# Layer 1's weight tiles at the end of a two-layer graph kernel: one of four made by GpSimd instead of VectorE

## The chip, the cores and the metric

The kernel runs on one core of a Trainium2 chip. The metric is the device time of one launch in microseconds. The engines are named as in the profile: PE is TensorE, with PEld its weight load; DVE is VectorE, ACT is ScalarE, POOL is GpSimd, and SP is SyncE, which here only issues transfers.

## The reference

Eight batches of 2048 nodes with 256 features pass through two layers over one adjacency matrix. After each layer comes a residual sum and a layer norm.

```python
# layer 0: attention within chunks of 256 keys, 4 heads of 64
scores = clip(einsum('bhnd,bhjcd->bhnjc', q, kc) / sqrt(64), -10, 10)
scores = where(mask == 0, -10.0, scores)
attn = softmax(scores, axis=-1)
ctx = einsum('bhnjc,bhjcd->bhnd', attn, vc)
out = layernorm(ctx @ Wo.T + bo + x) * gamma + beta
x = layernorm(x + out)
# layer 1: graph attention over all nodes, 4 heads of 64
Wh = (x @ W).reshape(B, N, 4, 64)
e = s_src[:, :, None, :] + s_dst[:, None, :, :]
e = where(e > 0, e, 0.2 * e)
e = where(adj != 0, e, -inf)
alpha = softmax(e, axis=2)
x = layernorm(x + elu(einsum('bijh,bjhd->bihd', alpha, Wh)))
```

## The kernel before

All tensors are in float32, apart from the masks, which are bytes. The order of instructions on every engine is written out by hand (a manual schedule): each engine runs its instructions in the order in which the program emits them, and waits only for what it needs.

**Layer 0** of a batch is a loop of 64 slots. A slot makes two tiles of scores on PE (L377), clips and masks them on DVE from PSUM into two `pr` buffers of 128 x 1024 (L388), takes the exponential on ACT (L400), multiplies by the values on PE (L412), and copies the result out on ACT (L419). POOL divides by the sums and adds up (L434 into `part` or `acc`, L436). The `pr` pool has four buffers.

**Layer 1** of a batch is cut into 12 units: three bands of 6, 5 and 5 blocks of 128 target nodes (`BANKS`), times four heads. A unit has 16 weight tiles, one for each block j of 128 source nodes. A tile is 128 x 768 in the first band and 128 x 640 in the others. The exponential of the leaky sum has been factored, so that a tile `e` is the maximum of a row `srow` (the same on all partitions) and a scalar `gd` per partition, times the adjacency bytes `et`. One DVE instruction makes it (L734), in `Layer1.make`. `Layer1.use` then takes the tile as the weights of 12 or 10 matrix products with `waug` (L754), which the profile records as 24 or 20. The `e` pool has four buffers. The bytes come by SP transfers of four tiles each (L716, `JG = 4`, three buffers), the rows by one transfer per unit (L705, two buffers).

When a unit is done, `close` takes the reciprocal of its sums on DVE (`dn`, L777 and L778), scales on ACT (`hh`, L782), applies the pieces of the elu (`ee` and `hp`, L786 and L788), and joins them on DVE (L790).

Layer 1 of batch b runs beside layer 0 of batch b + 1: `Layer1.step`, called once in each slot, makes and uses three tiles, with the tiles made three ahead of their use. For the last two batches this differs:

- In batch 7's layer 0 the last 14 slots (`LATE`) make no step of batch 6's layer 1. Those 14 steps are emitted afterwards, between the pieces that finish batch 7's layer 0 (output product, two norms, values for layer 1, and `factors`, whose last piece scales `waug` on POOL at L681).
- Layer 1 of batch 7 then runs with no layer 0 beside it: 64 steps of three tiles. Between them the final norms of batch 6 and of most of batch 7 are done: sum (L815), statistics (L477, L480), `rs_c` and `off_c` (L485 and L486 on DVE, L487 and L488 on POOL), and the scaled output `o` on ACT (L492), which SP stores (L821).

Of the kernel before, what the change touches and what calls it, by code (L numbers as in the profile page):

```python
# [8 lines left out]
F32 = mybir.dt.float32  # L9
# [5 lines left out]
ALU = mybir.AluOpType  # L15
AX = mybir.AxisListType

P = 128
CH = 512
# [3 lines left out]
def adj_resnorm_kernel(  # L23
# [19 lines left out]
    nc = tc.nc  # L43
# [26 lines left out]
    WIDE = max(BANKS)  # L70
    JG = 4
# [4 lines left out]
    prp = ctx.enter_context(tc.tile_pool(name="prp", bufs=4))  # L76
    ep = ctx.enter_context(tc.tile_pool(name="ep", bufs=4))
# [3 lines left out]
    small = ctx.enter_context(tc.tile_pool(name="small", bufs=2))  # L81
# [117 lines left out]
    class Masks:  # L199
# [3 lines left out]
        def __init__(self):  # L203
            self.pieces = [
                (QT * q + u, m) for q in range(NCH) for m in range(len(BANKS)) for u in range(QT)
            ]
            self.raw, self.bits, self.done = [], [], []
            self.next = 0
# [152 lines left out]
    def load_slab(s):  # L361
        q, hp, c = where[s]
        slab = slabs.tile([P, KT, CH], I8, tag="slab", name="slab")
        nc.sync.dma_start(out=slab, in_=clipD[q][:, KT * c : KT * (c + 1), :])
        slab_of[s] = slab

    def scores(s):
        q, hp, c = where[s]
        slab = slab_of.pop(s)
        cols = slice(q * CH, (q + 1) * CH)  # L370
        pss = []
        for u in range(KT):
            t = KT * c + u
            ps = two_banks([P, 2, CH], "ps")
            for k in range(2):
                rows = slice(k * D, (k + 1) * D)
                nc.tensor.matmul(  # L377
                    ps[:, k, :],
                    lhsT=kT[rows, hp, t * P : (t + 1) * P],
                    rhs=qT[rows, hp, cols],  # L380
                    start=True,
                    stop=True,
                )
            pss.append(ps)
        probs[s] = []
        for u in range(KT):
            pr = prp.tile([P, 2, CH], F32, tag="pr", name="pr")
            nc.vector.scalar_tensor_tensor(  # L388
                pr,
                pss[u],  # L390
                -CLIP,
                slab[:, u, :].unsqueeze(1).to_broadcast([P, 2, CH]),
                op0=ALU.max,
                op1=ALU.min,
            )
            probs[s].append(pr)

    def exps(s, u):
        pr = probs[s][u]
        nc.scalar.activation(pr, pr, AF.Exp, scale=0.125)  # L400
# [289 lines left out]
    class Layer1:  # L690
        def __init__(self, b, gd, waug):
            self.b, self.gd, self.waug = b, gd, waug
            self.made = self.used = 0
            self.rows, self.edge, self.e = {}, {}, {}
            self.tail = []
            self.load_edge(0)
            self.load_edge(1)
            self.load_row(0)
# [22 lines left out]
        def make(self):  # L721

            if self.made == TILES:
                return
            k = self.made
            n, j = k // NT, k % NT
            m, h = UNITS[n]
            if j == NT // 2:
                self.load_row(n + 1)
            if j % JG == 0:  # L730
                self.load_edge(k // JG + 2)
            w = BANKS[m] * P
            e = ep.tile([P, WIDE * P], F32, tag="e", name="e")
            nc.vector.scalar_tensor_tensor(  # L734
                e[:, :w],
                self.rows[n][:, :w],
                self.gd[:, h, j : j + 1],
                self.edge[k // JG][:, j % JG, :w],
                op0=ALU.max,
                op1=ALU.mult,  # L740
            )
            self.e[k] = e
            self.made += 1

# [160 lines left out]
    lower = None  # L905
    for b in range(B):
# [15 lines left out]
        for s in range(SLOTS):  # L922
            q, hp, c = where[s]
            i = s % QS
# [93 lines left out]
        if b + 1 < B:  # L1018
            (k0, v0, q0), (l1, t1, k1, v1, q1), (l2, t2, k2, v2, q2), (l3, t3, k3, v3, q3) = turns
            rest = [lambda: lower.rest(1)] if lower else []  # L1020
            first = [] if b else [lambda: before.values((1,))]
            order = [begin, *rest, l1, *rest, *first, lambda: before.values((2, 3))]
            order += [*rest, ctx, *rest, k0]
            order += [steps[0], t1, steps[1], v0, steps[2], steps[3], l2, k1, steps[4], q0]
            order += [steps[5], v1, t2, l3, steps[6], q1, steps[7], k2, steps[8], steps[9], t3, v2]
            order += [lambda: [load_slab(s) for s in range(3)], fs[0], q2, fs[1], k3, fs[2], v3]
            order += [lambda: scores(0), q3, lambda: [exps(0, u) for u in range(KT)]]
        else:

            step = lower.step  # L1030
            order = [begin, lambda: before.values((2, 3)), steps[0], step, ctx, step, steps[1], step]
            order += [steps[2], step, steps[3], step, steps[4], step, steps[5], step, steps[6], step]
            order += [steps[7], step, steps[8], step, steps[9], step, fs[0], step, fs[1], step, fs[2]]
            order += [step, lambda: lower.rest(4)]
            assert sum(p is step for p in order) == LATE
# [4 lines left out]
        lower = Layer1(b, gd, waug)  # L1040

    closing, ending = Closing(B - 2, CLOSING_ALONE), Closing(B - 1, ENDING)
    closing.do(-1)
    for _ in range(STEP):
        lower.make()
    for s in range(SLOTS + 1):
# [50 lines left out]
```

## Time and profile before

| | us |
|---|---|
| median of 3 runs (3795.84 to 3798.59) | 3796.66 |
| the profiled execution | 3792.69 |
| its span | 3790.9 |

| engine | busy us | share of the span | instructions |
|---|---|---|---|
| PE | 3678.4 | 97% | 72100 |
| DVE | 3195.5 | 84% | 4810 |
| ACT | 1946.8 | 51% | 3601 |
| POOL | 1387.7 | 37% | 1202 |

The profile is one execution. A row of a group has the line, the engine, the operation, output and inputs with their shapes, and the count; then busy time in all and the mean of one in ns; then the engine's idle time just ahead of these instructions and what ended it. A row of the timeline has the start in us from the beginning of the span, the length, the engine, the line and the count.

### The profile page before, as it was taken

Reading aid. Unit: us, or ns where it says so; the run is one execution under the profiler, and the core shown is the slowest. Engines: PE = TensorE matmul, PEld = TensorE weight load, DVE = VectorE, ACT = ScalarE, POOL = GpSimd, SP = SyncE. Lnnn points to the kernel's source line nnn. Section 1 sums busy time; section 2 is a strip of 40 time slices with the busy share of each in tenths; the row PEclk is TensorE's granted clock in tenths of the full one; section 3 lists DMA queues with packets and bytes.
Section 4 is the critical chain, followed back from the end, with each engine's and each line's share of the span. In section 5 each row is a group of like instructions: output and inputs, shape, how many; then the busy total and the mean of one; then the engine's idle time right before and its main releaser. Section 6 shows DMA issues by size and latency. Waiting matters only on the chain. (4 is left out here: it accounts for less than half of the span.)

```text
span 3790.9 us, 160217 instructions
## 1 busy us (share of the span) xinstructions
PE 3678.4 (97%) x72100; PEld 2747.7 (72%) x72100; DVE 3195.5 (84%) x4810; ACT 1946.8 (51%) x3601; POOL 1387.7 (37%) x1202
## 2 busy tenths in 40 slices
PE   9999999999999999999999999999999999999787
PEld 5656677776777777776777767777677777776676
DVE  5876499986999689995999959998699968998798
ACT  4666355545555555554555545555555555555221
POOL 1445234333444344333443324433344434434310
PEclk9999999999999999999999999999999999999899
DMA  6652334333343343433433434333333333343354
GB/s 164 152 114 67 76 102 105 100 82 113 106 105 101 89 120 98 104 96 87 137 86 104 102 99 126 105 100 82 113 106 104 101 88 120 98 104 81 97 152 120
DMA packets 756545, 398.50 MB, mean 105 GB/s; under 512 B 425744, under 2 KB 721040, under 8 KB 755856
## 3 DMA queue, kind: packets, MB, share of 16 engines
q1 hardware_dynamic: 705856, 354.54, 36.6%
q10 hardware_dynamic: 50000, 33.70, 2.8%
q8 instruction: 564, 9.24, 1.0%
q14 instruction: 125, 1.02, 0.1%
HBM read 331.22 MB, written 56.89 MB: 102 GB/s over the span
## 5 line engine op out<-in xcount | busy, mean ns | idle before, releaser
L388 DVE SCALAR_TENSOR_TENSOR pr<-ps,slab 128x1024 f32<-128x1024 f32 x1024 | 1191.3, 1204 | 199.2 <-PE ps L377 195.1
L734 DVE SCALAR_TENSOR_TENSOR e<-srow,gd,et 128x640 f32<-128x640 f32 (+1 forms) x1536 | 1342.6, 930 | 10.1 <-PE pa L754 5.4
L412 PEld LDWEIGHTS pc<-vaug,pr 128*64 128x64 f32 x32768 | 1039.7, 138 | 411.2 <-issue 303.6
L412 PE MATMUL pc<-vaug,pr 128*64 128x65 f32 x32768 | 1156.3, 224 | 17.6 <-ACT raw L419 10.0
L754 PE MATMUL pa<-waug,e 128*64 128x65 f32 x32768 | 1080.5, 224 | 39.6 <-DVE e L734 37.8
L400 ACT ACTIVATE pr<-pr 128x1024 f32<-128x1024 f32 x1024 | 1044.9, 1056 | 71.2 <-DVE pr L388 60.3
L754 PEld LDWEIGHTS pa<-waug,e 128*64 128x64 f32 x32768 | 1020.7, 139 | 63.8 <-DVE e L734 37.6
L377 PE MATMUL ps<-qT,kT 64*128 64x512 f32 x4096 | 1025.7, 617 | 3.3 <-DVE pr L388 2.4
L419 ACT COPY raw<-pc 128x260 f32<-128x260 f32 x1024 | 384.8, 376 | 1235.7 <-PE pc L412 1196.2
L434 POOL TENSOR_TENSOR part<-raw,rd 128x512 f32<-128x512 f32 x448 | 467.9, 1044 | 1424.5 <-DVE rd L427 1410.2
L377 PEld LDWEIGHTS ps<-qT,kT 64*128 64x128 f32 x4096 | 350.3, 186 | 328.1 <-issue 222.6
L436 POOL TENSOR_TENSOR acc<-acc,part 128x512 f32<-128x512 f32 x448 | 574.9, 1283 | 35.2
L427 DVE RECIPROCAL rd<-raw 128x8 f32<-128x8 f32 x512 | 100.5, 196 | 102.4 <-ACT raw L419 100.7
L434 POOL TENSOR_TENSOR acc<-raw,rd 128x512 f32<-128x512 f32 x64 | 66.7, 1043 | 317.4 <-DVE rd L427 316.6
L782 ACT ACTIVATE hh<-pa,dn 128x64 f32<-128x64 f32 x512 | 114.7, 322 | 101.5 <-DVE dn L778 101.5
L571 PE MATMUL pw<-w_sb,x1T 128*128 128x264 f32 x512 | 140.9, 411 | 9.2 <-DVE x1T L283 8.7
L487 POOL TENSOR_TENSOR rs_c<-rs_c,nhalf 128x4 f32<-128x4 f32 x32 | 55.6, 1737 | 229.6 <-DVE off_c L486 229.6
L321 PE MATMUL pp<-xT,wk_sb 128*128 128x512 f32 x256 | 118.6, 607 | 7.9 <-ACT qT L329 6.6
L527 PE MATMUL po<-wo_sb,qT 128*128 128x256 f32 x512 | 125.0, 389 | 1.1 <-DVE qT L454 0.8
L321 PE MATMUL pp<-xT,wq_sb 128*128 128x512 f32 x256 | 116.2, 596 | 0.0
L337 PE MATMUL pv<-wv_sb,xT 128*128 128x256 f32 x512 | 115.9, 379 | 0.0
L571 PEld LDWEIGHTS pw<-w_sb,x1T 128*128 128x128 f32 x512 | 92.9, 194 | 30.9 <-DVE x1T L283 9.3
(93 smaller groups left out, 1857.3 us busy)
## 6 DMA issues: line engine op xcount, KB each, us to landing
et<-edgeD SPq DMA_DIRECT2D x256, 320.0 KB, 3.1
slab<-clipD SPq DMA_DIRECT2D x512, 128.0 KB, 3.3
et<-edgeD SPq DMA_DIRECT2D x128, 384.0 KB, 3.4
srow<-rowD SPq DMA_DIRECT2D x64, 320.0 KB, 4.2
xg<-in_x_dram SPq DMA_DIRECT2D x32, 512.0 KB, 5.1
x1D<-y ACTq DMA_DIRECT2D x32, 512.0 KB, 4.2
x1g<-x1D SPq DMA_DIRECT2D x32, 512.0 KB, 5.3
out_dram<-o SPq DMA_DIRECT2D x32, 512.0 KB, 3.7
```

Source lines behind the costliest of these rows:

```text
L321: nc.tensor.matmul(pps[c], lhsT=w[:, kc, c * P : (c + 1) * P], rhs=st["xT"][:, kc, :], start=(kc == 0), stop=(kc == KC - 1),)
L377: nc.tensor.matmul(ps[:, k, :], lhsT=kT[rows, hp, t * P : (t + 1) * P], rhs=qT[rows, hp, cols], start=True, stop=True,)
L388: nc.vector.scalar_tensor_tensor(pr, pss[u], -CLIP, slab[:, u, :].unsqueeze(1).to_broadcast([P, 2, CH]), op0=ALU.max, op1=ALU.min,)
L400: nc.scalar.activation(pr, pr, AF.Exp, scale=0.125)
L412: nc.tensor.matmul(pc[z * D : (z + 1) * D, i, :], lhsT=probs[s][u][:, k, i * P + z * D : i * P + (z + 1) * D], rhs=vaug[:, KT * c + u, 2 * ...
L419: nc.scalar.copy(raws[s][:, k], pc)
L434: nc.gpsimd.tensor_mul(part, raw[:, :, :, :D], rd.to_broadcast([P, 2, QT, D]))
L436: nc.gpsimd.tensor_add(accv, accv, part)
L527: nc.tensor.matmul(po[:, k, :], lhsT=qT[:, c, t * P : (t + 1) * P], rhs=wo_sb[:, c, :], start=(c == 0), stop=(c == KC - 1),)
L571: nc.tensor.matmul(pw[:, k, : F + 2 * H], lhsT=self.x1T[:, c, u * P : (u + 1) * P], rhs=w1_sb[:, c, :], start=(c == 0), stop=(c == KC - 1),)
L734: nc.vector.scalar_tensor_tensor(e[:, :w], self.rows[n][:, :w], self.gd[:, h, j : j + 1], self.edge[k // JG][:, j % JG, :w], op0=ALU.max, ...
L754: nc.tensor.matmul(self.pa[z * D : (z + 1) * D, i * D1 : (i + 1) * D1], lhsT=e[:, i * P + z * D : i * P + (z + 1) * D], rhs=self.waug[:, j ...
```

## The change

A flag `shared` is added to `Layer1`. It is set for batch 6's layer 1 just before its last 14 steps are emitted, and for batch 7's layer 1 before its first tile. While it is set, the tiles with j % 4 = 2 are made in another way: ACT copies the bytes into floats, in a buffer of the `pr` pool that layer 0 no longer uses; POOL takes the maximum of the row and the scalar, in the buffer of `part`; and POOL multiplies the two. The other three of four tiles are made as before. The tile `e` of the shared ones takes no buffer of the `e` pool.

```diff
             w = BANKS[m] * P
-            e = ep.tile([P, WIDE * P], F32, tag="e", name="e")
-            nc.vector.scalar_tensor_tensor(
-                e[:, :w],
-                self.rows[n][:, :w],
-                self.gd[:, h, j : j + 1],
-                self.edge[k // JG][:, j % JG, :w],
-                op0=ALU.max,
-                op1=ALU.mult,
-            )
+            row, edge = self.rows[n][:, :w], self.edge[k // JG][:, j % JG, :w]
+            scalar = self.gd[:, h, j : j + 1]
+            if self.shared and j % JG == 2:
+
+                e = prp.tile([P, 2, CH], F32, tag="pr", name="eg").rearrange("p k i -> p (k i)")
+                nc.scalar.copy(e[:, :w], edge)
+                top = small.tile([P, WIDE * P], F32, tag="part", name="top", bufs=1)
+                nc.gpsimd.tensor_scalar(top[:, :w], row, scalar, None, ALU.max)
+                nc.gpsimd.tensor_mul(e[:, :w], e[:, :w], top[:, :w])
+            else:
+                e = ep.tile([P, WIDE * P], F32, tag="e", name="e")
+                nc.vector.scalar_tensor_tensor(
+                    e[:, :w], row, scalar, edge, op0=ALU.max, op1=ALU.mult
+                )
...
+            lower.shared = True
             step = lower.step
...
     closing.do(-1)
+    lower.shared = True
     for _ in range(STEP):
         lower.make()
```

More of the change, by code (lines that the diff above doesn't have):

```diff
@@ L693, in __init__ @@
             self.made = self.used = 0
+            self.shared = False
             self.rows, self.edge, self.e = {}, {}, {}
```

## The prediction

> **What bounds the kernel now.** I read the engine shares and the slices first, then the stretches at the end, then groups, waits and the order of time there. On the page PE is busy for 97% of the span and DVE for 84%; the change touches only tiles made after layer 0 has run out of work, so what counts is the last 270 us. The view by stretches gives, for each: length, busy us and instructions of PE, weight load, DVE, ACT, POOL, then granted clock, DMA share and GB/s.
>
> ```profile
> 3520.00:3585.00 65.00, 49.85 (x1004) 43.82 (x1000) 50.90 (x85) 19.34 (x53) 20.91 (x14) 0.88 0.34 99
> 3585.00:3662.00 77.00, 62.10 (x1580) 55.45 (x1582) 76.44 (x122) 15.02 (x40) 10.99 (x9) 0.90 0.47 143
> 3662.00:3775.00 113.00, 100.12 (x2520) 85.68 (x2520) 110.72 (x173) 20.67 (x68) 3.78 (x4) 0.97 0.49 135
> ```
>
> From 3585 to 3775 (the last batch's 192 weight tiles, alone) DVE is busy for 187 of 190 us, PE for 162, ACT for 36, POOL for 15. The groups and waits of 3590 to 3775 name the work: 188 tiles by L734 on DVE, with no idle time ahead of them, and PE waiting on them and on hardly anything else.
>
> ```profile
> L734 DVE SCALAR_TENSOR_TENSOR e<-srow,gd,et 128x640 f32<-128x640 f32 x128 | 103.2, 876 | 0.0
> L734 DVE SCALAR_TENSOR_TENSOR e<-srow,gd,et 128x768 f32<-128x768 f32 x60 | 56.6, 1009 | 0.0
> ...
> PE pa L754 <- DVE e L734: 23.1, 27, 3.6
> ```
>
> The rows of the timeline give the pace (start, length, engine, line, count):
>
> ```profile
> 3632.15 8.43 DVE L734 SCALAR_TENSOR_TENSOR e<-srow,gd,et 128x768 f32<-128x768 f32 x9
> 3633.20 8.35 PE L754 MATMUL pa<-waug,e 128*64 128x65 f32 x216 [0.29 <-DVE e L734]
> ...
> 3719.57 7.22 DVE L734 SCALAR_TENSOR_TENSOR e<-srow,gd,et 128x640 f32<-128x640 f32 x9
> 3720.48 7.17 PE L754 MATMUL pa<-waug,e 128*64 128x65 f32 x180 [0.27 <-DVE e L734]
> ```
>
> So in a row a tile costs DVE 7.22/9 = 0.80 us at 640 wide and 8.43/9 = 0.94 at 768, and PE 0.80 and 0.93. DVE sets the end here, PE is close behind: with DVE wholly free of the bound, only PE's 23 us of waiting could go.
>
> **What the Trainium skill says.** "SBUF — State Buffer", Who interferes with whom: a DVE instruction with two inputs in SBUF contends with a GpSimd instruction that reads SBUF; the shared pair of ports is an exclusive lock for the whole instruction, and the second to issue "fully blocks". L734 has two such inputs, the row srow and the bytes et. L388, layer 0's big DVE step, has one (ps lies in PSUM), so layer 0 tells nothing on this. "GPSIMD Engine Reference", Elementwise — side-by-side cycle accounting: about 2.6 cycles an element at 1.2 GHz for two inputs, 1.03 for a light one-input body, about 1.8 for a tight loop.
>
> The trace of before agrees on the lock, where waug is scaled on POOL beside L734. A POOL multiply of 1024 takes 1.90 us undisturbed (minimum of its line), a tile of 640 takes 0.84 to 0.88:
>
> ```profile
> 3575.43 0.88 DVE L734 SCALAR_TENSOR_TENSOR e<-srow,gd,et 128x640 f32<-128x640 f32 x1
> 3576.42 2.48 POOL L681 TENSOR_TENSOR waug<-waug,ed 128x1024 f32<-128x1024 f32 x1
> 3577.06 2.52 DVE L734 SCALAR_TENSOR_TENSOR e<-srow,gd,et 128x640 f32<-128x640 f32 x1
> ```
>
> The multiply that starts at 3576.42 ends at 3578.90, some 1.8 us after the tile ahead of it (about 3577.1); the tile issued at 3577.06 ends at 3579.58, 0.68 us after the multiply. Neither shares: they take turns, a POOL instruction held the pair for about its own time less 0.1 (its start-up overlaps the wait), and a tile behind one costs 0.68 instead of 0.80 (I take 0.82 for 0.94 at 768). The same stands at 3527, where a tile took 1.67 us beside a POOL multiply.
>
> **The change part by part.**
>
> Removed: one L734 in four, from the point where the flag is set. The flag comes with 14 steps of batch 6's layer 1 to go: tiles 153 to 191 are then still to be made, 10 of them with j % 4 = 2, all 640 wide. Of the last batch's 192, 48 are: 16 of 768, 32 of 640. DVE's saving alone is 32 x 0.80 + 16 x 0.94 = 40.6 us for the last batch and 8.0 ahead of it.
>
> Added on ACT: 58 copies of bytes into floats. The nearest row, L242's casts (685 ns at 640, 790 at 768), makes 58 of them about 42 us. ACT is busy for 36 of 190 us in the last stage, and needs neither lock nor DVE: I cost them at nothing beside the DVE-POOL turns. If that cover were gone, at most 42 us would show. ACT is in order: behind a copy stand hh, ee and hp of L782 to L788 and the o rows of L492; a copy itself stands behind hh (which waits for dn on DVE) and behind o (which waits for POOL's off_c). Tiles are ordered three ahead of PE, about 2.4 us, so one such wait is mostly borne; I bound it from 0 to 1.5 us at each of six norms, 0 to 9, and take 0.
>
> Added on POOL: 58 maxima and 58 multiplies, all reading SBUF. No row shows a POOL maximum at this shape: by the skill's 1.03 cycles an element plus 0.2 us of start (estimate; the 64-element copy of L679 takes 0.30), 0.75 us at 640 and 0.86 at 768; by 1.8 cycles, 1.14 and 1.33. I take the lower. Multiply: L436, with two full inputs, takes 1283 ns at 512; less 0.18 of start that is 2.15 ns an element, which is the skill's 2.6 cycles; so 1.56 us at 640 and 1.83 at 768. By L434 and L681, with a broadcast input (1044 at 512, 1903 at 1024, 1.68 an element), 1.26 and 1.47. I take the higher. Held less 0.1 each: 2.11 us a tile at 640, 2.49 at 768.
>
> A group of four tiles, DVE and POOL in turns:
> - at 640, before 4 x 0.80 = 3.20; after 0.68 + 0.68 + 0.80 + 2.11 = 4.27, so 1.07 longer;
> - at 768, before 3.75; after 0.82 + 0.82 + 0.94 + 2.49 = 5.07, so 1.32 longer.
>
> Last batch: 32 x 1.07 + 16 x 1.32 = 55 us. Against it stand DVE instructions with fewer than two SBUF tensors, beside which POOL can run: statistics 8.4 + 2.2, rs and off 2.0, dn 4.1, in all 16.7 us; I count half, 8. Leaves 47. The 10 tiles ahead of it: 10 x 1.07 = 11; DVE has 14 of 65 us idle there, so I count 6. Sum **+53 us**.
>
> Moved: eg uses layer 0's pr buffers, four of them, once in four tiles, so a buffer is free 16 tiles later, and its wait costs nothing; e's own four buffers now last 5.3 tiles. top takes part's buffer, used by POOL alone, in order. A transfer of bytes now waits for ACT's read too, and one of rows for POOL's; three byte buffers of four tiles leave room, and the SP queue (et, srow, x1g, out) is paced by the tiles as now: nothing. On POOL rs_c and off_c stand behind up to a maximum and a multiply, about 2.3 us; o behind them isn't wanted at once. The waug multiplies stand behind one tile of batch 6, which PE needs first anyway. The last 15 us (3775 on) have no such tile and stay. PE: 3.2 us of work in 4.27 leaves gaps of about 1 us; the granted clock, 0.90 to 0.97 here now, may dip; PE has room for it.
>
> The profiled execution took 3792.7 us (span 3790.9 and 1.8 around it); 3792.7 + 53 = 3845.7. The median of the runs, 3796.7, is 4 above the profiled time, so I forecast **3850 us**.
>
> **The rivals.**
> - *Turns, at higher prices or with queues in the way.* Maximum at 1.8 cycles: 4.66 and 5.54 us a group, 32 x 1.46 + 16 x 1.79 = 75, nothing covered, 15 ahead, 9 in ACT's queue: about +99, 3895. For it: POOL has no one-input row of this width. I give 0.2.
> - *Turns, cheap.* Multiply by the broadcast rows: 3.97 and 4.71 a group, 32 x 0.77 + 16 x 0.96 = 40, less all 16.7 of cover and nothing ahead: +23, 3820. 0.15.
> - *Faster: PE becomes the bound.* POOL works beside DVE, the group takes PE's 3.2 us, and most of PE's 23 us of waiting goes, with perhaps 5 ahead of it: about 3770. It decides from where both POOL instructions hold the pair for less than one DVE tile and the two shortened ones, 0.80 + 0.24 = 1.04 us at 640. One 512-wide multiply alone takes 1.04, and the 2.52 us tile above speaks against it; for it speaks that POOL runs beside DVE all through layer 0 (L434 at 1044). 0.07.
> - *Nothing to see*, losses and cover cancelling: 0.03.
>
> **How the numbers follow.** The main case has 0.55. Range 3818 to 3895: it spans the cheap and dear ends and leaves out the faster and the level case and a tail above. A measurement of this kernel can tell about 0.2% (8 us) from no change: faster 0.07, same 0.03, slower 0.90.
>
> **What would show it.** L734 falls by 58; surviving tiles of the end have means well over 0.88 and 1.01 us, many at 1.5 to 2.5; POOL's new rows have means above their undisturbed prices; stage 3585 to 3775 grows to about 237 us with DVE still reported nearly full and PE waiting longer for e and eg. Wrong would be: tiles at 0.84 beside POOL rows at full width, or PE waiting for ACT's copies rather than for POOL and DVE.

## The result and the profile after

The change makes the kernel slower: 3864.9 us median (3863.7 to 3868.4) against 3796.3, a ratio of 1.0183 with a 95% interval of 1.0171 to 1.0196, or +68.6 us. The forecast was 3850, with a range of 3818 to 3895.

The page of the changed kernel puts the loss at the very end. These are the busy rows in 40 slices (a digit is the share in tenths), DVE and POOL before, then DVE and POOL after.

```profile
DVE  5876499986999689995999959998699968998798
POOL 1445234333444344333443324433344434434310
...
DVE  5876599977999599995999779995999959986898
POOL 1444234333434244433443334332443424446897
```

In the last four slices POOL is busy for 60% to 90% and more, where it had 40% falling to nothing before, and DVE is no emptier for it. The stretch of the last batch's tiles, from the start of the first to the end of the last product, before and after (length; busy us and instructions of PE, weight load, DVE, ACT, POOL; granted clock, DMA share, GB/s):

```profile
3585.40:3773.80 188.40, 162.21 (x4096) 141.13 (x4096) 186.45 (x293) 35.21 (x105) 14.66 (x12) 0.94 0.48 139
...
3597.40:3846.00 248.60, 161.24 (x4096) 147.05 (x4096) 228.17 (x244) 66.55 (x151) 223.13 (x109) 0.89 0.37 107
```

PE's busy time for its 4096 recorded products is 161 us against 162, so the granted clock, 0.89 instead of 0.94, is not where the time went. A tile has three ways to be late now: DVE, POOL, or ACT's copy. The groups and PE's waits of the last batch (3590 to 3847 us) show which:

```profile
L745 DVE SCALAR_TENSOR_TENSOR e<-srow,gd,et 128x640 f32<-128x640 f32 x96 | 125.0, 1363 | 3.9 <-PE pa L760 3.9
L741 POOL TENSOR_SCALAR top<-srow,gd 128x640 f32<-128x640 f32 x32 | 75.3, 2353 | 3.0
L745 DVE SCALAR_TENSOR_TENSOR e<-srow,gd,et 128x768 f32<-128x768 f32 x48 | 72.8, 1572 | 4.7 <-PE pa L760 4.6
L742 POOL TENSOR_TENSOR eg<-eg,top 128x640 f32<-128x640 f32 x33 | 58.0, 1757 | 4.9 <-issue 1.9 <-POOL top L741 0.4
...
PE pa L760 <- POOL eg L742: 58.6, 37, 8.0
PE pa L760 <- DVE e L745: 33.9, 32, 7.5
```

DVE makes 144 tiles of the last batch instead of 192, but a tile of 640 takes 1363 ns in the mean instead of 876. Its busy time for tiles rose from some 163 us to 198. PE waits 92 us instead of 23, and no wait for ACT's copy is among the waits of that stretch.

One group of four tiles, row by row of the timeline (start, length, engine, line), shows why. In the kernel before, four such tiles took 3.20 us.

```profile
3834.13 1.69 POOL L742 TENSOR_TENSOR eg<-eg,top 128x640 f32<-128x640 f32 x1
3834.36 2.15 DVE L745 SCALAR_TENSOR_TENSOR e<-srow,gd,et 128x640 f32<-128x640 f32 x1
3835.92 2.33 POOL L741 TENSOR_SCALAR top<-srow,gd 128x640 f32<-128x640 f32 x1
3836.43 1.42 DVE L745 SCALAR_TENSOR_TENSOR e<-srow,gd,et 128x640 f32<-128x640 f32 x1
3837.77 0.87 DVE L745 SCALAR_TENSOR_TENSOR e<-srow,gd,et 128x640 f32<-128x640 f32 x1
3838.34 1.69 POOL L742 TENSOR_TENSOR eg<-eg,top 128x640 f32<-128x640 f32 x1
```

The next group begins 4.20 us after this one (3834.13 to 3838.34). Follow the ends. The multiply ends at 3835.82, and the tile issued beside it ends 0.69 later, at 3836.51. The maximum then gets its turn. The next tile ends at 3837.85, and since a tile behind a turn needs 0.68, its turn began at 3837.17: the maximum had kept DVE out for only 0.66 us, though it goes on until 3838.25. The third tile, 0.87 us, runs undisturbed beside the rest of the maximum and ends at 3838.64. Then the second multiply keeps the ports until 3840.03. The turns are 0.69 + 0.66 + 0.68 + 0.79 + 1.39 = 4.21 us. That they add up without a gap follows from how they are counted, each from the end of the one before. What is not by count is how regular they are: in this trace all 30 DVE tiles of 640 that start while a multiply of 640 runs end 0.68 to 0.69 us after it, as the tile at 3834.36 does. With the maximum none does: the tile that waits for it ends some 0.41 us before the maximum's own end.

By stages, in the two profiled executions (72.2 us apart): 3.3 us lie ahead of batch 7's last pieces, before any changed instruction (nothing is changed there in the ten kernels below either, and their profiled executions take 2.0 to 7.9 us longer for it than the one before). From there to the first tiles of the last batch, with 10 shared tiles, it takes 67.7 us instead of 59.0 (+8.7). The last batch's tiles take 248.6 us instead of 188.4 (+60.2). From the last matmul to the end it takes 17 us in both.

### The profile page after: what moved, and what is told of

Its sections match the earlier page's. It is cut to its first block, busy times and chain, and to the rows that moved or that the text cites. A ratio compares the mean times of both kernels' runs of the same rounds, so it can differ in the third digit from the quotient of the medians.

```text
span 3862.8 us, 160403 instructions
## 1 busy us (share of the span) xinstructions
PE 3678.7 (95%) x72100; PEld 2753.8 (71%) x72100; DVE 3237.9 (84%) x4752; ACT 1985.6 (51%) x3659; POOL 1633.5 (42%) x1318
## 5 line engine op out<-in xcount | busy, mean ns | idle before, releaser
L745 DVE SCALAR_TENSOR_TENSOR e<-srow,gd,et 128x640 f32<-128x640 f32 (+1 forms) x1478 | 1374.8, 985 | 22.4 <-PE pa L760 16.6
L760 PE MATMUL pa<-waug,e 128*64 128x65 f32 x31544 | 1037.4, 224 | 38.3 <-DVE e L745 37.3
L760 PEld LDWEIGHTS pa<-waug,e 128*64 128x64 f32 x31544 | 985.6, 140 | 49.9 <-DVE e L745 36.4
L741 POOL TENSOR_SCALAR top<-srow,gd 128x640 f32<-128x640 f32 (+1 forms) x58 | 142.2, 2451 | 4.8
L760 PE MATMUL pa<-waug,eg 128*64 128x65 f32 x1224 | 52.4, 239 | 70.9 <-POOL eg L742 70.9
```

The lines of the kernel that those rows point to most:

```text
L741: nc.gpsimd.tensor_scalar(top[:, :w], row, scalar, None, ALU.max)
L745: nc.vector.scalar_tensor_tensor(e[:, :w], row, scalar, edge, op0=ALU.max, op1=ALU.mult)
L760: nc.tensor.matmul(self.pa[z * D : (z + 1) * D, i * D1 : (i + 1) * D1], lhsT=e[:, i * P + z * D : i * P + (z + 1) * D], rhs=self.waug[:, j ...
```

## Experiments

Two theories lead to a slower kernel. **A, turns:** POOL and DVE take turns at the SBUF ports that they share, so the time of POOL's reads is added to DVE's tiles. **B, POOL's queue:** POOL is simply too slow for one tile in four. In the trace after, both look full (POOL is busy for 223 of the 248.6 us, DVE for 228), so these shares alone do not tell them apart.

### Take the second SBUF input away from DVE: e1_rows_psum, e2_rows_psum_all_dve

```diff
+            near = row
+            if self.alone:
+                if k == 0:
+                    self.bring(0)
+                if j == NT - 4:
+                    self.bring(n + 1)
+                near = self.near[n][:, :w]
...
+        def bring(self, n):
...
+                self.near[n] = two_banks([P, 2, CH], "near").rearrange("p k i -> p (k i)")
+                nc.scalar.copy(self.near[n][:, :w], self.rows[n][:, :w])
...
-                    e[:, :w], row, scalar, edge, op0=ALU.max, op1=ALU.mult
+                    e[:, :w], near, scalar, edge, op0=ALU.max, op1=ALU.mult
```

> The changed kernel, but in the last batch's layer 1 ACT copies each unit's row into PSUM (two banks that layer 0 no longer uses) and DVE's tiles read it there; POOL goes on reading the row in SBUF. A DVE tile then has one SBUF input. Theory A (turns for the shared ports set the pace, 4.20 us a group of four at 640 wide): the tiles fall back to 0.85 to 0.9 us, POOL's maximum and multiply to their undisturbed 1.88 and 1.53, and the pace becomes POOL's own 3.6 us a group at 640, 4.2 at 768: 48 groups 182 us, with 28 us for POOL's norm steps and their waits 210 against 249 in the changed kernel, so about 3826 us. Theory B (POOL's queue by itself sets it, the ports don't matter): 3865, nothing moves. Theory C (only the ports matter): PE's pace, about 3785.

> Control for the run before: the kernel before, all tiles on DVE, with the last batch's rows in PSUM. If a tile costs DVE the same from PSUM (two L388 of 1024 take 2.34 us, as much per element as SBUF to SBUF), 3797 within 5. If PSUM rows cost by themselves, more: 0.06 us a tile for 192 tiles would be 12.

In both, ACT copies each unit's row into PSUM once, and DVE's tiles of the last batch read it there (`near`). e1 took 3816.7 us (3813.3 to 3818.8), a ratio to before of 1.0051 (1.0036 to 1.0066): 48 us less than the changed kernel, by nothing but the place of DVE's row. The control e2 took 3794.9, a ratio of 0.9993 (0.9985 to 1.0002), so PSUM rows by themselves are neither gain nor loss. In e1's timeline the tiles and POOL's instructions have their undisturbed lengths side by side:

```profile
3748.83 1.88 POOL L756 TENSOR_SCALAR top<-srow,gd 128x640 f32<-128x640 f32 x1
...
3750.80 1.54 POOL L757 TENSOR_TENSOR eg<-eg,top 128x640 f32<-128x640 f32 x1
3751.28 0.88 DVE L760 SCALAR_TENSOR_TENSOR e<-near,gd,et 128x640 f32<-128x640 f32 x1
3752.08 0.88 DVE L760 SCALAR_TENSOR_TENSOR e<-near,gd,et 128x640 f32<-128x640 f32 x1
3752.44 1.89 POOL L756 TENSOR_SCALAR top<-srow,gd 128x640 f32<-128x640 f32 x1
```

The group now takes 3.61 us (3748.83 to 3752.44), which is POOL's own 1.88 + 1.54 with two gaps of 0.1. So A holds for the 48 us, and B for a rest: without turns POOL is still slower than PE's 3.2 us. In the profiled executions the last batch takes 200.9 us in e1, 248.6 in the changed kernel and 188.4 before, so 12.5 us of 60.2 are left to B there. The remainder of e1's loss is the 10 early tiles, whose rows e1 leaves in SBUF. A's forecast of 3826 was 9 too high, by the same 9 as its 210 us for the last batch. A theory in which only the ports matter would have put e1 near 3785. e1's waits in the last batch (3600 to 3797 us) agree: PE waits for POOL and hardly for DVE.

```profile
PE pa L775 <- POOL eg L757: 58.8, 46, 2.6
PE pa L775 <- DVE e L760: 0.5, 1, 0.5
```

### Take half of POOL's work away: e3_no_max

```diff
-                top = small.tile([P, WIDE * P], F32, tag="part", name="top", bufs=1)
-                nc.gpsimd.tensor_scalar(top[:, :w], row, scalar, None, ALU.max)
-                nc.gpsimd.tensor_mul(e[:, :w], e[:, :w], top[:, :w])
+                nc.gpsimd.tensor_mul(e[:, :w], e[:, :w], row)
```

> The changed kernel with POOL's maximum left out: POOL multiplies the floats by the row itself, so a shared tile lacks the maximum. Theory A (turns): a group at 640 takes 0.68 + 0.80 + 0.80 + 1.39 = 3.67 us against 3.20 before, at 768 about 4.4 against 3.75: 32 x 0.47 + 16 x 0.65 = 25 us more than before for the last batch and up to 5 ahead of it, less up to 10 of cover: 3810 to 3827. Theory B (POOL's queue alone): POOL needs 1.7 us a group, PE becomes the bound, 3770 to 3785, faster than before.

3823.1 us (3822.2 to 3829.9), ratio 1.0073 (1.0058 to 1.0088), inside A's interval and 38 us or more above B's. POOL has time to spare here and DVE has none, by the groups of the last batch (3605 to 3811 us):

```profile
L743 DVE SCALAR_TENSOR_TENSOR e<-srow,gd,et 128x640 f32<-128x640 f32 x96 | 116.5, 1276 | 0.0
...
L740 POOL TENSOR_TENSOR eg<-eg,srow 128x640 f32<-128x640 f32 x32 | 63.5, 1999 | 54.7 <-ACT eg L739 46.8 <-PE pa L758 7.8
```

The kernel is slower than before although POOL's 32 multiplies have 55 us of idle time ahead of them and DVE has a quarter fewer tiles: the tiles that are left have become half as long again. And the maximum is worth (3864.9 - 3823.1) / 58 = 0.72 us a tile, close to the 0.66 that it kept DVE out and far from its own 1.88. The 0.72 has in it whatever POOL's queue costs besides, so the two agree only roughly.

### ACT's part by itself: e4_act_copies

```diff
-                nc.gpsimd.tensor_scalar(top[:, :w], row, scalar, None, ALU.max)
-                nc.gpsimd.tensor_mul(e[:, :w], e[:, :w], top[:, :w])
-            else:
+            if True:
```

> The kernel before with all tiles on DVE, and ACT's 58 copies of bytes into floats kept, which nothing reads. If ACT's part is free as predicted: 3797 within 3. If copies delay hh, o and with them dn and the norms, up to 42 us (58 x 0.73).

3796.0 us, ratio 0.9997 (0.9988 to 1.0006): the 58 copies cost nothing that can be measured.

### Where, and how many: e5_late_only, e6_one_in_eight

The edits drop the flag for the last batch, or put `j % 8 == 2` for `j % JG == 2`.

> The changed kernel with the sharing only in batch 6's last 14 steps (10 tiles); the last batch's tiles are all on DVE. By the prediction 6 us more than before, by the changed kernel's profile 8.7: 3803 to 3808. If the part ahead of the last batch hides its tiles altogether, 3797.

> The changed kernel with one tile in eight on POOL instead of one in four, rows in SBUF. Theory A (each shared tile adds its turns): half the loss, 3825 to 3835. Theory B (POOL's queue sets the pace only because POOL has too many tiles): POOL needs some 4 us in eight tiles of 6.4, so PE or DVE sets it, and DVE has one tile in eight less: 3780 to 3790.

e5: 3805.5, ratio 1.0025 (1.0016 to 1.0034), so the 10 early tiles cost 9.3 us. e6: 3831.3, ratio 1.0091 (1.0076 to 1.0106), so half of the tiles cost half of the loss: 35 us for 29 tiles, 1.21 each, and 68.6 for 58, 1.18 each. POOL's multiplies of 640 have 45 us of idle time ahead of them in e6, and every shared tile still costs its turns. With B the half would have been a gain.

### From the reason to a faster version: e7 to e10

If turns are the reason, then without them a share small enough for POOL should gain. All four runs have the row for DVE in PSUM and share nothing ahead of the last batch. e7 gives POOL one tile in eight. e8 gives it one in four, but lets ACT make the maximum, as the positive part of row minus scalar, plus the scalar (`neg` is the scalar with its sign turned, made once on DVE):

```diff
-                nc.gpsimd.tensor_scalar(top[:, :w], row, scalar, None, ALU.max)
+                nc.scalar.activation(top[:, :w], row, AF.Relu, bias=neg)
+                nc.scalar.activation(top[:, :w], top[:, :w], AF.Identity, bias=scalar)
```

> The last batch's rows for DVE in PSUM, one tile in eight on POOL, nothing shared ahead of the last batch. Theory A: no turns, POOL has 3.6 us of work in eight tiles of 6.4, DVE seven tiles and its 29 us of norms, 168 us against 188 before: 3775 to 3785. If what is left of the contention (sums and joins with two SBUF inputs, POOL's latency) eats it: 3790 to 3797.

> The last batch's rows for DVE in PSUM, one tile in four shared, nothing shared ahead of the last batch; of the shared tile ACT makes the maximum too (Relu of row minus scalar, then plus scalar), POOL only multiplies. Theory A: POOL 1.6 us, ACT 2.1 us, DVE 2.4 us and PE 3.2 us in a group of four, so PE sets the pace: 3770 to 3780. If ACT's four instructions a group delay dn, hh and the row copies: 3785 to 3800.

e7: **3781.3 us** (3779.6 to 3785.7), ratio 0.9960 (0.9945 to 0.9975), faster than both kernels. e6 has the same share and takes 50 us more; what sets it apart from e7 is its rows in SBUF and five early tiles (half of e5's 9.3 us), so the rows are worth some 45. e8 missed the gain: 3797.5, ratio 1.0003 (0.9994 to 1.0011). Its waits name a ring between ACT and POOL:

```profile
POOL eg L759 <- ACT top L758: 72.7, 35, 4.8
...
ACT top L757 <- POOL eg L759: 21.9, 24, 1.4
```

`top` has one buffer. ACT can't begin the next maximum before POOL has multiplied with this one, and POOL waits for ACT. The period in the timeline is 3.40 us, 0.83 + 0.83 + 1.55 and the handovers. e9 gives `top` two buffers (`tag="acc"`, whose pool holds two). e10 goes on from e7 with three tiles of 16.

> The run with ACT making the maximum, but with two buffers for it instead of one. In the trace of that run ACT's Relu waited for POOL's multiply of the group before, and the multiply for ACT: 0.83 + 0.83 + 1.55 + handovers = 3.40 us a group at 640. If that ring is the cause, PE's 3.2 us sets the pace: 9 to 14 us less, 3783 to 3789. If ACT's order (o, hh and row copies between) is the cause, no change: 3795 to 3800.

> Rows for DVE in PSUM, three tiles of 16 on POOL (j = 2, 7, 12) instead of two, last batch only. In the run with one in eight PE still waited 17 us for DVE. Theory A: DVE has 12 tiles less, 10 us; POOL's 36 tiles take 137 us plus norms: PE sets the pace, 3772 to 3780. If POOL's latency of 3.6 us a tile is late for PE at that spacing: 3782 to 3792.

e9: 3783.0, ratio 0.9966 (0.9954 to 0.9979), 14.5 us less than e8 by the second buffer alone. Whether e7 or e9 is better stays open: in the profiled executions e9's last batch is the shorter, 170.5 us against 177.1 in e7 and 188.4 before, but 7.9 us more than before had gone by in it where nothing was changed.

e10: 3787.6, ratio 0.9976 (0.9970 to 0.9983), no better than e7 and most likely worse (the two intervals overlap a little). Its waits have changed sides: between 3600 and 3775 us PE waits 22.5 us for POOL and 6.3 for DVE, where e7 had 4.5 and 16.7. A POOL tile takes 3.6 us, and PE comes to it after four or five tiles of 0.8 us; POOL also stands 16 us at `rs_c`, waiting for DVE's statistics. That these two make POOL's tile late is read from the waits, no run separates them.

## Why the prediction was right, and where its sizes were off

- **The bound before** (DVE, tiles of 0.80 and 0.94 us) and what could be gained at most were read right: the best version gains 15 us of the 23 that PE waited.
- **The turns** were read right from the few places where POOL worked beside L734. e1 shows the mechanism, e3 and e6 show that POOL's queue is not the main part. The Trainium skill's page "SBUF — State Buffer" (Who interferes with whom) is confirmed on who contends, also on a DVE instruction with one SBUF input being free (e1). Its statement that the lock is held for the whole instruction is not: by the rows above the maximum kept DVE out for 0.66 us of its undisturbed 1.88. The measurement decides. The prediction had named tiles of 0.84 us beside POOL rows as a sign that it was wrong; the third tile of the group above, 0.87 us, is such a tile, beside the second half of the maximum.
- **The price of a group** came out at 4.20 us (forecast 4.27) at 640, and 4.98 at 768, between the maxima that start at 3658.97 and 3663.95 (forecast 5.07). The multiply was priced well: 1.54 us undisturbed at 640, forecast 1.56. The maximum was not: 1.88 where the prediction took 0.75, from a price of 1.03 cycles an element that does not hold for it here. The sum survived by luck: what counts in turns is the time for which DVE is kept out, and 0.66 happened to be near the 0.65 used.
- **The term that was missing is POOL's own queue, and what a late tile of POOL does to DVE.** For the last batch the forecast was 55 us of turns less 8 of cover (statistics beside which POOL can run), 47, all of it in DVE's busy time. That time grew by 41.7 us (186.45 to 228.17). The other 18.5 of the 60.2 are time in which DVE stands idle, 20.4 us instead of 2. For 19.4 of these it waits for PE:

```profile
DVE dn L783 <- PE pa L760: 10.8, 3, 5.8
DVE e L745 <- PE pa L760: 8.6, 2, 4.6
...
POOL rs_c L487 <- DVE off_c L486: 13.7, 4, 5.4
```

Ahead of each of these five waits PE itself had waited for a tile of POOL. In four of them POOL had made the steps `rs_c` and `off_c` of a norm shortly before that tile, and in three it had first stood 3.4 to 5.4 us until DVE's statistics were there. The prediction saw that these steps would wait behind a tile, and put that at nothing; it did not see that the tiles behind them would wait too. With a maximum of 1.88 us POOL's chain is 1.88 + 1.54 + 0.2 = 3.6 us a tile undisturbed, which leaves it little to catch up with: it was busy or waiting at `rs_c` for 237 of 248.6 us. That the long maximum is what used up its slack is argued from these numbers, no run isolates it.
- **The tiles ahead of the last batch**: 6 forecast, 9.3 measured (e5); the idle time of DVE there covered almost nothing of the 11.
- **ACT's copies and the moved buffers at nothing**: e4 shows it for the copies; no wait of note on `eg`'s or `top`'s buffers is in the trace after. The sum was +53, the runs gave +68.6: some 13 in the last batch (60.2 against 47), 3 ahead of it.

## What to carry to other kernels

Before moving work from DVE to POOL, look at what the remaining DVE instructions read. Here, with two SBUF inputs, they took turns with POOL, and the sum of the turns, not the fuller of the two engines, set the pace. A mean that grows on the engine that was relieved (876 to 1363 ns here), with next to no idle time ahead of it, is how this looks in a profile; both engines full and a consumer waiting for both is its other mark. One input moved to PSUM ended it at no measurable cost (e1, e2), and then the share has to fit the slower engine's own time. Look also at what else stands in that engine's queue, since a tile behind it waits with it.

## What the runs showed of the hardware that was not expected

- POOL's maximum of a row with a scalar per partition takes 1.88 us at 640 and 2.20 at 768 (e1 and e7 have it undisturbed), longer than its multiply of two tensors (1.54 and 1.81, e1). At 640 it shut DVE out for only about a third of that (0.66 us by the rows of the group above).
- A DVE tile whose row lies in PSUM takes, within 0.5%, as long as one with its row in SBUF: 873 and 1005 ns in e2, 876 and 1009 before.
